# A gated cross-attention block: block 1's queries from a transposed copy in DRAM, quantized tokens transposed by TensorE, and a reordered start and end

## The chip, the cores and the metric

The kernel runs on one core of a Trainium2 chip. The metric is the time of one execution on the device, in microseconds (us). The engines work side by side and wait for one another through semaphores: TensorE (PE in the profile; PEld is its weight load), VectorE (DVE), ScalarE (ACT), GpSimd (POOL) and SyncE (SP), which here only issues transfers.

## What is computed

```python
# x: (2, 2048, 512), ctx: (2, 77, 512), all float32
n = layernorm(x)
q, k, v = n @ Wq.T + bq, ctx @ Wk.T + bk, ctx @ Wv.T + bv     # 16 heads of 32
a = softmax(q @ k.T / sqrt(32)) @ v
x = x + tanh(g_xattn) * (a @ Wo.T + bo)

def qlinear(x, w, b):            # one scale for a whole tensor
    sx, sw = max(abs(x)) / 127, max(abs(w)) / 127
    return (round(x / sx) @ round(w / sw).T + b) * (sw * sx)

h = gelu(qlinear(layernorm(x), w1, b1))      # 512 -> 2048
x = x + tanh(g_ffn) * qlinear(h, w2, b2)     # 2048 -> 512
```

A scale is the largest value over all tokens. So no token can be quantized before the attention of the last one is done, and the second layer can't begin before the last value of `h` is known.

## The kernel before

The 4096 tokens are cut into 8 blocks (`NB`) of 512 tokens (`TB`), each of 4 tiles of 128 (`NT`). Blocks 0 to 3 belong to the first batch entry, 4 to 7 to the second. Three stages follow each other: attention over all blocks, the first feed-forward layer over all blocks, the second over all blocks.

**Attention.** Its order is written out by hand for all five engines: each engine runs its instructions in the order of the source. A block has 8 steps `s`; one step handles one group of 4 heads and half of the block's tokens. In step `k = 8i + s` the loop at L805 does this: `shares` of step k+1 (sum of the exponentials, reciprocal, and on POOL the product `e*rs`, L566), the products that a table assigns to the step (`plan`, `second`, `begin`, `end`), `apply_v` for a finished group, `scores` of step k+2 with their minimum `mx` on DVE (L537), the 8 transposes `pta` of the step's `e` on PE (L577) with two copies by ACT, the exponentials of step k+2 on ACT (L548), and then other work: sums for the products, norms of later blocks, preparation of the weights w1 and w2 (`tasks`). The projections of queries and outputs use seven products of quarters (`unit_q`, `unit_o`) whose sums POOL makes; blocks 0 and 1 project their queries plainly (`project_q`, L350).

Where the queries come from: for block 0 and 1 `normalize` (L332) makes the normalized tokens `xn` on DVE and `transpose_x` (L339) turns them round on PE with a copy by ACT. From block 2 on the kernel loads the transposed input `xT` from DRAM and `scale_x` (L303) multiplies it on POOL by a row of 1/sigma; the mean is taken care of by `center_wq` (L324), which subtracts from wq its column means. The row takes a round trip: `write_row` (L290) writes the 512 values of `rstd` to DRAM from SP, `read_row` (L295) reads them back to all 128 partitions.

The start (L776 to L802): norms and transposes of block 0 tile by tile, with the keys of batch entry 0 (`project_k`, L232; `place_k`, L245, puts the four heads of a group with four small instructions into `kblk`), then queries, scores of steps 0 and 1, and the values (`project_v`). The keys and values of batch entry 1 follow in steps 3 to 6 of block 0 (L909). `bank` (L224) hands out two PSUM banks in turn (`pp0`, `pp1`) to `project_k`, `project_q`, `project_v`, `project_o` and `pm`: a new tile waits until the last reader of the tile before in its bank is done. Transfers go through SP's queue in order of the source. x, the raw weights and wk and wv share 8 buffers of 1 MB (`big`, L74), so the last of the four loads of w1 waits for the last use of wk (L236). POOL's first small instruction, `nbk` (L777), needs `bk`, and `inverse_sigma` (L170) runs behind it.

The end of attention: block 7 hands its work on by halves (`apply_v_half`, L597). Steps 5 to 7 project the outputs of tile 0, 1, and of tiles 2 and 3 in parts; behind the loop follow the last group, the extremes of each token (`extreme`, L642), the norms, and the common scale (`scale_of`, L185).

**First feed-forward layer** (L1014): for each block 16 chunks of 128 hidden units, 4 matmuls of 128x512 each in bf16 (L1031), one Gelu by ACT (L1039) out of four PSUM banks (`ps_h`), and one `tensor_reduce` by DVE for the largest value of each two chunks (L1049). `G` holds 4 chunks; there are 10 such tiles, the last 10 are kept, the others are stored to DRAM. Meanwhile `quantize_x` (L996) makes the next block's tokens: DVE normalizes, scales and rounds them (two tiles at a time) and DMA transposes (L1010), issued by SP, turn them round. Only PE's order is written by hand here; a scheduler places the rest.

**Second layer** (L1072): ACT and DVE quantize `h`, held or read back, PE multiplies (L1098), and the results go out.

Of the kernel before, what the change touches and what calls it, by code (L numbers as in the profile page):

```python
# [15 lines left out]
P = 128  # L16
D = 512
# [25 lines left out]
def tile_flamingo_gated_block(  # L43
# [88 lines left out]
    for g in range(2, NG):  # L132
        load_group(nc.sync, wq_sb, wqT, g)
    for b in range(1, B):
        load_ctx(nc.sync, b)
    load_x(1)
# [5 lines left out]

    nc.sync.dma_start(wo_sb, kchunks(woT))
# [10 lines left out]
    nc.vector.memset(ones, 1.0)  # L154
    mhalf = const.tile([P, NT], F32, name="mhalf")
# [6 lines left out]
    hmax = const.tile([P, NB * GT * 2 + 1], F32, name="hmax")  # L162
# [55 lines left out]
    with actx:  # L218
# [97 lines left out]
        def sum_columns(total):  # L316

            pm = bank("pm")
            nc.tensor.matmul(pm, ones, total, start=True, stop=True)
            mean = work.tile([P, D], F32, tag="rrow", name="wq_mean", bufs=1)  # L320
            nc.scalar.activation(mean, pm, AF.Copy, scale=1.0 / D)
            return mean
# [27 lines left out]
        def project_q(i, g):  # L350
            pq = bank(f"pq{i}_{g}")
            for kc in range(KC):
                nc.tensor.matmul(  # L353
                    pq,
                    wq_sb[:, kc, g * P : (g + 1) * P],
                    (xnT if i < 2 else xT_sb)[i][:, kc, :],
                    start=(kc == 0),
                    stop=(kc == KC - 1),
                )
            if g % 2 == 0:  # L360
                qT[i, g // 2] = work.tile([P, 2, TB], F32, tag="qT", name=f"qT{i}_{g}", bufs=2)
            q = qT[i, g // 2][:, g % 2, :]
            nc.scalar.activation(q, pq, AF.Identity, bias=bq_sb[:, g : g + 1])
# [149 lines left out]
        def part(i, s):  # L513


            return divmod(s, 2) if i + 1 < NB else (s % NG, s // NG)

        def scores(i, s):

            g, half = part(i, s)  # L520
            n = f"{i}_{s}"

            ps = ps_s.tile([P, NR, 512], F32, tag="ps", name=f"ps{n}")
            for u in range(2):
                t = 2 * half + u
                for q in range(NR):
                    r = slice(q * RT * DK, (q + 1) * RT * DK)
                    nc.tensor.matmul(  # L528
                        ps[:, q, u * RK : (u + 1) * RK],
                        qT[i, g // 2][r, g % 2, t * P : (t + 1) * P],  # L530
                        kblk[i // NBB][r, g, :],
                        start=True,
                        stop=True,
                    )
            mx = small.tile([P, NR, 2, RT], F32, tag="mx", name=f"mx{n}")
            sc = ps[:, :, : 2 * RK].rearrange("p q (u r k) -> p q u r k", u=2, r=RT)
            nc.vector.tensor_reduce(mx, sc, AX.X, ALU.min)  # L537
            scored[i, s] = sc, mx
# [58 lines left out]
        def apply_v_half(i, s):  # L597

            g, half = part(i, s)
            odd = s % 2  # L600
            pc = ps_t.tile([P, H], F32, tag="pt", name=f"pc{i}_{s}")
            for j in range(HG):
                r = slice(j * DK, (j + 1) * DK)
                c = g * P + j * DK
                nc.tensor.matmul(
                    pc[r, :],
                    vblk[i // NBB][:, c : c + DK],
                    aT[i, s // 2][:, j, odd * H : (odd + 1) * H],
                    start=True,
                    stop=True,  # L610
                )
            if s in (0, 2):
                cT[i, g // 2] = work.tile([P, 2, TB], F32, tag="cT", name=f"cT{i}_{g}", bufs=3)
            nc.scalar.copy(cT[i, g // 2][:, g % 2, half * H : (half + 1) * H], pc)
# [135 lines left out]
        begin = {1: ("", "p2"), 3: ("", "p3"), 5: ("", "P0"), 6: ("", "P1"), 7: ("", "P2")}  # L750
# [25 lines left out]
        nbk = small.tile([P, KC], F32, tag="nbk", name="nbk", bufs=1)  # L776
        nc.gpsimd.tensor_scalar(nbk, bk_sb, -SCALE, None, ALU.mult)  # L777
        pk = {}
        for t in range(NT + 1):
            if t < NT:  # L780
                norm_stats(0, t)
            if t > 0:
                normalize(0, t - 1)
                transpose_x(0, t - 1)
            if t in (2, 3):
                pk[t - 2] = project_k(0, t - 2)
        place_k(0, 0, pk[0])
        pk[2] = project_k(0, 2)
        place_k(0, 1, pk[1])
        project_q(0, 0)  # L790
        place_k(0, 2, pk[2])
        pk[3] = project_k(0, 3)
        place_k(0, 3, pk[3])
        load_x(2)
        for j in range(4):
            load_w("w1", j)
        for s in range(2):
            scores(0, s)
            exponential(0, s)
        project_q(0, 1)  # L800
# [4 lines left out]
        for i in range(NB):  # L805
# [3 lines left out]
            for s in range(2 * NG):  # L809
# [22 lines left out]
                if i == 0:  # L832
                    if s == 1:
                        total = sum_wq()
                    if s == 2:


                        nc.scalar.activation(tg, tg, AF.Tanh)
                        nc.gpsimd.tensor_scalar(bo_sb, bo_sb, tg[:, 0:1], None, ALU.mult)
                    if s in (5, 6):  # L840
                        for n in range(2):
                            sums_wq(2 * (s - 5) + n)
                    if s == 7:
                        for n in range(2):
                            sums_wo(n)
                if i == 1 and s in (1, 2):
                    sums_wo(s + 1)
                if i > 0 and s < 2:
                    for n in ((1, 2), (4,))[s]:
                        sums_c(i - 1, n)  # L850
                if more and i > 0:
# [5 lines left out]
                for t in range(NT):  # L857
                    if s == ((4, 5, 6, 7) if i == 0 else (4, 4, 5, 6))[t]:
# [4 lines left out]
                if i == 0 and s in (2, 3):  # L863
                    normalize(1, 2 * s - 4)
                    normalize(1, 2 * s - 3)
# [8 lines left out]
                if i > 0:  # L874
# [4 lines left out]
                    these = {5: (0,), 6: (1,), 7: (2,)} if more else {6: (0, 1), 7: (2,)}  # L879
# [11 lines left out]
                if not more and s > 4:  # L891

                    if s < 7:
                        project_o(i, s - 5)
                        later = [(add_o, i, s - 5), (norm2_stats, i, s - 5)]
                    else:
                        both = ps_s.tile([P, NR, 512], F32, tag="ps", name="po_last")
                        for these in (0, 1), (2,):
                            project_o(i, 2, these)
                            for n, c in enumerate(halves):  # L900
                                project_o(i, 3, these, c, psum=both[:, n, :])
                if i == 0 and s == 2:
                    mean = sum_columns(total)
                if i == 0 and s == 3:
                    center_wq(mean)
                if i == 0 and s in (3, 4):
                    transpose_x(1, 2 * s - 6)
                    transpose_x(1, 2 * s - 5)
                if i == 0 and 3 <= s < 7:  # L909
                    for b in range(1, B):  # L910
                        place_k(b, s - 3, project_k(b, s - 3))
                        if s == 6:
                            project_v(b)
                for task, args in tasks.get(k, ()):
                    task(*args)
                if i + 2 < NB:
# [8 lines left out]
        i, last = NB - 1, range(NG - 1, NG)  # L925
# [4 lines left out]
        project_o(i, 2, last)  # L930
        for c in halves:
            project_o(i, 3, last, c)
        for n in range(3, 2 * NT):
            extreme(i - 1, n)
        for t in range(2):
            norm2_max(i, t)
        add_o(i, 2)
        norm2_stats(i, 2)
        norm2_max(i, 2)
# [50 lines left out]
    with ExitStack() as fctx:  # L990
# [3 lines left out]
        )  # L994

        def quantize_x(i):  # L996

            xqT = xqT0
            if i % 2:
                xqT = fwork.tile([P, KC, TB], BF16, tag="xqT", name=f"xqT{i}", bufs=1)  # L1000
            n = NT // 2
            for t0 in range(0, NT, n):
                xs = fwork.tile([P, n, D], F32, tag="xs", name=f"xs{i}_{t0}")
                xq = fwork.tile([P, n, D], BF16, tag="xq", name=f"xq{i}_{t0}")
                for t in range(n):
                    normalize2(xs[:, t, :], i, t0 + t)
                quantize(xq, xs, inv_x)
                for t in range(n):
                    r = slice((t0 + t) * P, (t0 + t + 1) * P)
                    nc.sync.dma_start_transpose(xqT[:, :, r], xq[:, t, :])  # L1010
            return xqT

        fctx.enter_context(tc.manual_schedule(engines={mybir.EngineType.PE}))
        for i in range(NB):  # L1014
            cur = xqT if i else xqT0
            if i + 1 < NB:
                with tc.issue_after(last):
                    xqT = quantize_x(i + 1)
            for a in range(GT):
                G = gtile(f"G{i}_{a}")  # L1020
                for v in range(GF // 2):
# [24 lines left out]
                    k = (i * GT + a) * 2 + v  # L1046
                    n = 1 if k == NB * GT * 2 - 1 else 2
                    for u in range(0, 2, n):
                        nc.vector.tensor_reduce(  # L1049
                            hmax[:, k + u : k + u + 1],  # L1050
                            G[:, 2 * v + u : 2 * v + u + n, :],
# [136 lines left out]
```

## Time and profile before

| | us |
|---|---|
| median of 3 runs (630.91 to 632.41) | 631.1 |
| the profiled execution | 631.38 |
| its span, first to last instruction | 629.5 |
| PE busy | 596.9 (95%) |
| DVE busy | 478.3 (76%) |
| ACT busy | 411.3 (65%) |
| POOL busy | 330.6 (53%) |
| first matmul of the first layer | 396.4 |
| second layer at full pace | from 517.8 |

Busy time is the time in which an engine ran an instruction. It is an average over stages, and an engine that is busy is not for that the one that sets the end: that is read from the waits and from the chain that ended last, of which PE has 80%. A PSUM tile or an SBUF tile that is used again makes its writer wait for the last reader, so a wait can lead back through several engines.

### The profile page before, as it was taken

What the parts mean: (1) busy time and instruction counts of PE and PEld (TensorE: products, weight loads), DVE (VectorE), ACT (ScalarE), POOL (GpSimd) and SP (SyncE); (2) the same over time, 40 slices, a digit from 0 to 9 for tenths busy, and PEclk for the clock granted to TensorE, in tenths of its full rate; (3) what the DMA queues carried; (4) which work ended last, traced back from release to release, by engine and by line L of the source; (5) the groups of instructions that cost most, each with busy time, mean ns of one, the idle gap of its engine ahead of it and who ended that gap; (6) DMA issues with size and microseconds to landing.
All of it is one profiled execution on the core that took longest, in us unless ns stands there. A gap on an engine that the chain in (4) does not pass through costs nothing.

```text
span 629.5 us, 9452 instructions
## 1 busy us (share of the span) xinstructions
PE 596.9 (95%) x3322; PEld 370.1 (59%) x3322; DVE 478.3 (76%) x743; ACT 411.3 (65%) x926; POOL 330.6 (53%) x291
## 2 busy tenths in 40 slices
PE   3999999899999999999999997899999979999997
PEld 3556467677778777777777744344444424444444
DVE  4476658668998788778666868999999789877452
ACT  1377556777766867866766653698999879555620
POOL 3076687679777799697885462000000009997000
PEclk9999999999999999999999999799999989999999
DMA  9910350041360053240000040399998019798932
GB/s 288 374 54 1 135 133 18 1 151 67 134 218 1 18 180 124 84 168 1 17 1 1 2 151 0 108 334 342 342 345 232 1 60 376 272 367 320 399 127 83
DMA packets 51270, 94.95 MB, mean 151 GB/s; under 512 B 22219, under 2 KB 26571, under 8 KB 45464
## 3 DMA queue, kind: packets, MB, share of 16 engines
q1 hardware_dynamic: 50120, 93.67, 43.6%
q10 hardware_dynamic: 1104, 0.69, 0.4%
q8 instruction: 26, 0.43, 0.3%
q14 instruction: 20, 0.16, 0.2%
HBM read 57.11 MB, written 33.57 MB: 144 GB/s over the span
## 4 chain that ended last, share of the span: by engine, by line
PE 80%; DVE 9%; ACT 4%; POOL 4%; issue 1%; DMA 1%; ACTq 0%; POOLq 0%; DVEq 0%
PE ph L1031 18%; PE pf L1098 17%; PE pta L577 8%; PE oa L443 6%; PE ps L528 5%; PE qa L443 5%; PE ob L443 5%; PE qb L443 4%; PE pc L586 3%; PE pq L353 3%; ACT e L548 2%; PE po L621 2%; PE pvv L261 1%; POOL cs L380 1%; DVE sm L562 1%
## 5 line engine op out<-in xcount | busy, mean ns | idle before, releaser
L566 POOL TENSOR_TENSOR e<-e,rs 128x616 f32<-128x616 f32 x64 | 77.8, 1216 | 95.7 <-DVE rs L564 89.3
L548 ACT ACTIVATE e<-ps,mx 128x77 f32<-128x77 f32 x512 | 116.9, 343 | 9.9 <-DVE mx L537 9.7
L1098 PE MATMUL pf<-w2q,hq 128*128 128x512 bf16 (+1 forms) x528 | 112.4, 376 | 2.5 <-DVE hq L212 2.3
L1031 PE MATMUL ph<-xqT,w1q 128*128 128x512 bf16 x512 | 112.4, 383 | 1.8 <-DVE xqT L212 1.8
L1039 ACT ACTIVATE G<-ph,b1s,s 128x512 f32<-128x512 f32 x128 | 99.2, 777 | 13.6 <-PE ph L1031 2.9
L578 ACT COPY aT<-pta 77x512 f32<-77x512 f32 x128 | 68.8, 587 | 53.4 <-PE pta L577 53.4
L1098 PEld LDWEIGHTS <-hq 128*128 128x128 bf16 x528 | 51.8, 98 | 63.0 <-DVE hq L212 3.1
L1031 PEld LDWEIGHTS <-w1q 128*128 128x128 bf16 x512 | 50.5, 99 | 63.6 <-issue 4.3
L1049 DVE TENSOR_REDUCE hmax<-G 128x1 f32<-128x1024 f32 (+1 forms) x65 | 76.9, 1197 | 7.0 <-ACT G L1039 6.9
L577 PE MATMUL pta<-ident,e 128*77 128x128 f32 x512 | 71.2, 281 | 2.9 <-POOL e L566 1.3
L1089 POOL TENSOR_SCALAR b_sb<-b_sb,s 128x512 f32<-128x512 f32 x1 | 3.5, 3493 | 122.1 <-issue 122.1
L562 DVE TENSOR_REDUCE sm<-e 128x8 f32<-128x616 f32 x64 | 50.4, 787 | 22.7 <-ACT e L548 22.5
L537 DVE TENSOR_REDUCE mx<-ps 128x8 f32<-128x616 f32 x64 | 50.2, 785 | 22.7 <-PE ps L528 22.5
L1091 ACT ACTIVATE Gb<-Gb,inv_h 128x2048 f32<-128x2048 f32 x22 | 43.6, 2000 | 31.9 <-DMA Gb<-h 30.8
L577 PEld LDWEIGHTS pta<-ident,e 128*77 128x77 f32 x512 | 55.5, 147 | 14.8 <-issue 8.0
L528 PEld LDWEIGHTS ps<-kb,qT 64*128 64x128 f32 x512 | 36.0, 186 | 37.1 <-issue 31.4
L1112 POOL TENSOR_TENSOR x<-x,b_sb 128x512 f32<-128x512 f32 x32 | 57.2, 1825 | 0.1
L528 PE MATMUL ps<-kb,qT 64*128 64x154 f32 x512 | 50.6, 317 | 0.7 <-DVE qT L489 0.4
L1120 DVE SCALAR_TENSOR_TENSOR x<-pf,s,x 128x512 f32<-128x512 f32 (+1 forms) x33 | 23.7, 729 | 34.6 <-PE pf L1098 26.8
L647 DVE TENSOR_REDUCE xm<-x 128x1 f32<-128x512 f32 x64 | 40.8, 669 | 0.0
L348 POOL TENSOR_TENSOR x<-x,bo_sb 128x512 f32<-128x512 f32 x32 | 40.4, 1272 | 0.0
L1092 DVE TENSOR_SCALAR hq<-Gb 128x2048 bf16<-128x2048 f32 x22 | 36.5, 1701 | 1.2 <-ACT Gb L1091 1.1
(146 smaller groups left out, 939.9 us busy)
## 6 DMA issues: line engine op xcount, KB each, us to landing
h<-G SPq DMA_DIRECT2D x22, 1024.0 KB, 5.2
Gb<-h SPq DMA_DIRECT2D x22, 1024.0 KB, 7.8
out_y<-x SPq DMA_DIRECT2D x31, 256.0 KB, 3.1
x<-in_x SPq DMA_DIRECT2D x7, 1024.0 KB, 6.9
xT<-in_xT SPq DMA_DIRECT2D x6, 1024.0 KB, 9.0
raw_w<-in_w2T SPq DMA_DIRECT2D x6, 1024.0 KB, 6.6
raw_w<-in_w1T SPq DMA_DIRECT2D x4, 1024.0 KB, 12.5
w_dram<-xqT SPq DMA_DIRECT2D x4, 512.0 KB, 3.3
```

The source lines that it names most:

```text
L443: nc.tensor.matmul(ps[:, m * H : (m + 1) * H], a[:, c, m * P : (m + 1) * P], b[:, c, :], start=(m + c == 0 and not more), stop=(m + c == 2 ...
L528: nc.tensor.matmul(ps[:, q, u * RK : (u + 1) * RK], qT[i, g // 2][r, g % 2, t * P : (t + 1) * P], kblk[i // NBB][r, g, :], start=True, sto ...
L548: last = nc.scalar.activation(es[i, s][:, u, j * NK : (j + 1) * NK], sc[:, q, u, r, :], AF.Exp, bias=mx[:, q, u, r : r + 1], scale=-1.0,)
L562: nc.vector.tensor_reduce(sm, e4, AX.X, ALU.add)
L566: return nc.gpsimd.tensor_tensor(e4, e4, rs[:, :, :, None].to_broadcast([P, 2, HG, NK]), ALU.mult).ins
L577: nc.tensor.transpose(pt[:NK, j, :], es[i, s][:, u, j, :], ident)
L578: nc.scalar.copy(aT[i, g][:, :, t * P : (t + 1) * P], pt[:NK, :, :])
L1031: nc.tensor.matmul(ph[u], w1q[:, kc, fc * P : (fc + 1) * P], cur[:, kc, :], start=(kc == 0), stop=(kc == KC - 1),)
L1039: nc.scalar.activation(G[:, 2 * v + u, :], ph[u], AF.Gelu, bias=b1s[:, fc : fc + 1], scale=s1,)
L1049: nc.vector.tensor_reduce(hmax[:, k + u : k + u + 1], G[:, 2 * v + u : 2 * v + u + n, :], AX.XY, ALU.max, apply_absolute_value=True,)
L1098: nc.tensor.matmul(po[t, c.start][:, : c.stop - c.start], hq[:, fc, t * P : (t + 1) * P], w2q[:, fc, c], start=(fc == 0), stop=(fc == FC - 1),
L1112: nc.gpsimd.tensor_tensor(y, y, b2_sb, ALU.add)
```

## The change

It has these parts.

- Loads: `load_x(1)` is issued ahead of wq's groups 2 and 3, and the transposed tokens of block 1 (`load_xT(1)`) ahead of wo. The fourth load of w1 moves to the tasks of step 5.
- Start: 21 transposes `run_up` of the identity into a PSUM tile before anything else on PE, and 3 more behind block 0's first tile. `nbk` moves behind the loop over the tiles. Behind `place_k(0, 0)` come queries and scores; groups 1 to 3 of the keys are placed behind the scores of steps 0 and 1.
- Block 1: its queries come from `xT_sb`, scaled by `scale_x(1, kc)` in step 3, with `write_row(1)` in step 1 and `read_row(1)` in step 2. `normalize(1, ..)` and `transpose_x(1, ..)` are gone. `center_wq` moves from step 3 to step 2, the last `project_q` of block 0 too (`begin`). Keys and values of batch entry 1 are made in steps 3 and 4 in place of 3 to 6. `sums_wq` and `add_bias` of blocks 0 and 1 move to other steps.
- Block 7: steps 4 to 7 take two groups of heads for one tile in place of one group for two tiles (`part`), so that tile 2 is complete one step before tile 3. Tile 2's output is projected whole in step 7; the extremes of block 6 move from behind the loop into steps 4 and 5.
- First layer: `transpose_q` turns the quantized tokens round with PE's transposes in bf16, 8 for each half of a block, ahead of the matmuls of `a = 2` and `a = 3`, into one of two new PSUM banks (`ps_q`), and ACT copies each half with one instruction. The DMA transposes are gone. The largest value of `h` is taken once for 4 chunks, but for the last tile.

```diff
+    load_x(1)
     for g in range(2, NG):
         load_group(nc.sync, wq_sb, wqT, g)
...
-    load_x(1)
+    load_xT(1)
...
-                    (xnT if i < 2 else xT_sb)[i][:, kc, :],
+                    (xT_sb if i else xnT)[i][:, kc, :],
...
-            return divmod(s, 2) if i + 1 < NB else (s % NG, s // NG)
+            if i + 1 < NB:
+                return s // 2, 2 * (s % 2) + u
+            return (s, u) if s < NG else (2 * (s % 2) + u, s // 2)
...
-        begin = {1: ("", "p2"), 3: ("", "p3"), 5: ("", "P0"), 6: ("", "P1"), 7: ("", "P2")}
+        begin = {1: ("", "p2"), 2: ("", "p3"), 5: ("", "P0"), 6: ("", "P1"), 7: ("", "P2")}
...
-        nbk = small.tile([P, KC], F32, tag="nbk", name="nbk", bufs=1)
-        nc.gpsimd.tensor_scalar(nbk, bk_sb, -SCALE, None, ALU.mult)
+        run_up = ps_s.tile([P, KC, P], F32, tag="ps", name="run_up")
+        for n in range(21):
+            nc.tensor.transpose(run_up[:, n % KC, :], ident, ident)
...
+            if t == 1:
+                for n in range(3):
+                    nc.tensor.transpose(run_up[:, n, :], ident, ident)
             if t in (2, 3):
                 pk[t - 2] = project_k(0, t - 2)
+        nbk = small.tile([P, KC], F32, tag="nbk", name="nbk", bufs=1)
+        nc.gpsimd.tensor_scalar(nbk, bk_sb, -SCALE, None, ALU.mult)
         place_k(0, 0, pk[0])
-        pk[2] = project_k(0, 2)
-        place_k(0, 1, pk[1])
         project_q(0, 0)
-        place_k(0, 2, pk[2])
-        pk[3] = project_k(0, 3)
-        place_k(0, 3, pk[3])
         load_x(2)
-        for j in range(4):
+        for j in range(3):
             load_w("w1", j)
+        at(5, load_w, "w1", 3)
         for s in range(2):
             scores(0, s)
             exponential(0, s)
+        place_k(0, 1, pk[1])
+        for g in range(2, NG):
+            place_k(0, g, project_k(0, g))
         project_q(0, 1)
...
+                    if s == 3:
+                        for kc in range(KC):
+                            scale_x(1, kc)
...
-                    if s == ((4, 5, 6, 7) if i == 0 else (4, 4, 5, 6))[t]:
+                    if s == ((5, 5, 6, 6) if i == 0 else (5, 6, 6, 7) if i == 1 else (4, 4, 5, 6))[t]:
                         add_bias(i, t)
...
-                if i == 0 and s in (2, 3):
-                    normalize(1, 2 * s - 4)
-                    normalize(1, 2 * s - 3)
...
-                    these = {5: (0,), 6: (1,), 7: (2,)} if more else {6: (0, 1), 7: (2,)}
+                    these = {5: (0,), 6: (1,), 7: (2,)} if more else {4: (0, 1, 2, 3), 5: (4, 5, 6, 7)}
...
                 if i == 0 and s in (3, 4):
-                    transpose_x(1, 2 * s - 6)
-                    transpose_x(1, 2 * s - 5)
-                if i == 0 and 3 <= s < 7:
                     for b in range(1, B):
-                        place_k(b, s - 3, project_k(b, s - 3))
-                        if s == 6:
+                        for n in ((0, 1, 2), (3,))[s - 3]:
+                            place_k(b, n, project_k(b, n))
+                        if s == 4:
                             project_v(b)
...
+                if k == 1:
+                    write_row(1)
+                    at(k + 1, read_row, 1)
...
-                    nc.sync.dma_start_transpose(xqT[:, :, r], xq[:, t, :])
...
+        def transpose_q(xqT, i, half, xq):
+
+            r = slice(half * HT * P, (half + 1) * HT * P)
+            pt = ps_q.tile([P, KC, HT, P], BF16, tag="pq", name=f"ptq{i}_{half}")
+            for u in range(HT):
+                for kc in range(KC):
+                    nc.tensor.transpose(pt[:, kc, u, :], xq[:, u, kc * P : (kc + 1) * P], ident16)
+            pt = pt.rearrange("p k u t -> p k (u t)")
+            nc.scalar.copy(xqT[:, :, r], pt)
...
+                if a >= 2 and i + 1 < NB:
+                    transpose_q(xqT, i + 1, a - 2, xq[a - 2])
...
-                    k = (i * GT + a) * 2 + v
-                    n = 1 if k == NB * GT * 2 - 1 else 2
-                    for u in range(0, 2, n):
+                    final = (i, a) == (NB - 1, GT - 1)
+                    k = i * GT + a + (2 * v if final else 0)
+                    for n, part_of in (
+                        ((0, slice(2 * v, 2 * v + 2)),) if final and v == 0
+                        else ((0, slice(2, 3)), (1, slice(3, 4))) if final
+                        else ((0, slice(0, GF)),) if v else ()
+                    ):
```

## The prediction

> **What bounds the kernel now.** I read the busy time by stage first, then TensorE's list of waits, then the timeline of the stages that the change touches.
>
> ```profile
> 0.00:31.70 31.70, 21.42 (x96) 14.27 (x96) 13.22 (x35) 8.46 (x23) 7.02 (x19) 1.00 0.98 331
> 31.70:81.00 49.30, 46.03 (x261) 26.26 (x259) 32.89 (x60) 33.38 (x103) 34.15 (x30) 1.00 0.17 59
> 81.00:136.00 55.00, 52.70 (x324) 39.23 (x322) 39.72 (x70) 36.52 (x106) 41.86 (x37) 1.00 0.26 68
> ...
> 381.00:396.40 15.40, 8.68 (x47) 5.71 (x46) 12.56 (x30) 5.04 (x9) 2.39 (x6) 0.89 0.00 0
> 396.40:507.90 111.50, 111.50 (x509) 50.19 (x509) 103.35 (x123) 97.97 (x127) 0.00 (x0) 0.98 0.76 241
> ```
>
> Columns: stretch, length, then busy us of PE, PEld, DVE, ACT, POOL, the clock, DMA share, GB/s. PE is the bound nearly everywhere. In the first feed-forward layer (396.4 to 507.9) it has no gap at all: whatever PE is given there is paid in full, whatever is taken from the DMA there is worth nothing. Gaps to win lie in the prologue (10.3 us), blocks 0 and 1 (3.3 and 2.3) and the turn at 381 (6.7).
>
> ```profile
> PE ptx L344 <- DVE xn L335: 10.1, 1, 10.1
> ...
> PE ph L1031 <- DVE xqT L212: 1.8, 1, 1.8
> PE qa L443 <- POOL xt L380: 1.6, 1, 1.6
> ```
>
> These are who PE waits for, with total us, times, longest: one long wait at the start, one of 1.6 us in block 1, and in L1031 only the first.
>
> **Prologue.** The timeline of before:
>
> ```profile
> 8.30 0.23 POOL L777 TENSOR_SCALAR nbk<-bk_sb 128x4 f32<-128x4 f32 x1 [5.90 <-DMA bk_sb<-in_bk]
> 9.54 0.55 DVE L335 TENSOR_SCALAR xn<-x,mv,rstd 128x512 f32<-128x512 f32 x1 [3.93 <-POOL rstd L175]
> 12.30 1.83 PE L236 MATMUL pk<-ctx,wk_sb 128*128 128x77 f32 x8
> 18.25 3.64 PE L353 MATMUL pq<-xnT,wq_sb 128*128 128x512 f32 x8
> 21.73 1.01 PE L236 MATMUL pk<-ctx,wk_sb 128*128 128x77 f32 x8
> 24.03 1.51 DVE L537 TENSOR_REDUCE mx<-ps 128x8 f32<-128x616 f32 x2
> 30.98 0.79 PE L528 MATMUL ps<-kb,qT 64*128 64x154 f32 x8
> ```
>
> nbk holds Pool, and rstd behind it, until bk lands. Moved behind the loop, rstd follows mv (4.82) by 0.24 + 0.57, so xn0 starts at 5.8 and xn3 ends 4.4 later as before, at 10.2. The same pk work takes 1.83 us at 12.3 and 1.01 at 21.7: PE runs at half speed until about 17.3, some 7 us after its first work at 10.14. The 21 run_up transposes start when ident is ready (1.9) and at the slow pace (four ptx in 0.9) end at 6.6. Full speed 7 us after 2 gives: ptx0 7.5, three more 8.2, ptx1 9.1, pk0 10.1, ptx2 10.6, pk1 11.6, ptx3 12.2, copy 0.6: pq0 at 12.8, against 18.25. Bounds: 11.9 if fast from 6.6, 15.2 if slow throughout.
>
> [...]
>
> But 5.4 us at pq0 don't reach the loop. The two banks of ps_p go in turn: pk2 takes the one of pk1, whose four place_k copies now stand behind both score minima on DVE. From pq0's start: scores 4.4 to 5.7, minima 5.3 to 6.8, place_k(0,1) 1.22 to 8.0, pk2 to 9.05, its copies to 10.3, and pq1, which takes that bank, 10.4 to 13.85, pvv, and scores 2 at 17.35 (before: 12.73). So scores 2 start at 30.15, not 30.98: 0.8 us won (1.9 won to 1.5 lost).
>
> **Block 0.** Removed: 16 ptx (0.13 each, 2.1 us of PE), four normalize, four copies; pk and pvv of the second batch move up. Added: four scale_x (1.27 each) on Pool behind a round trip through DRAM, and Pool multiplies e behind them. The DMA queue of before:
>
> ```profile
> 116.74 0.37 SPq L293 DMA_DIRECT2D row<-rstd  x1
> 125.12 0.34 SPq L299 DMA_DIRECT2D rrow<-row  x1
> ...
> 249.90 0.54 SPq L293 DMA_DIRECT2D row<-rstd  x1
> 261.90 0.34 SPq L299 DMA_DIRECT2D rrow<-row  x1
> ```
>
> The read is issued when the write has landed: 8.4 us in a quiet queue, 12 beside a load; the read lands in 3.3 to 5.9. xT1 (1 MB, 2.9 us at the 360 GB/s of then) goes early and the loads end at about 37, so I take 8.4 and 3.3 to 4.6. w1's fourth load no longer blocks SP until L236 is done with wk (70.6), or the write couldn't be issued. Counted from scores 2: step 0 and 1 as before, rstd at 11.9, pq3 10.4 to 13.9, mean at 15.4, center on Pool (4 x 1.33) to 20.75, e4 to 22.0; scales in hand at 23.7 to 25.1; scale_x 5.05 to 28.8 or 30.2; e5 1.22. PE runs pta3, three pk (the third waits for a bank to 19.85), pc, scores 6, pta4, pk, pvv and scores 7 to 28.8 and waits for e5 until 30.1 to 31.5: a new wait of 1.3 to 2.7 us. pq0 of block 1 starts at 31.8, or 61.95 (before 58.25). Up to the end of pq3 before took 27.1 us with two pk and a pvv (5.4) that are now done: 21.7, so 83.65 against 85.35: 1.7 us won by here (3.4 won to 2.9 lost: both bounds of the start, round trip up to 12 + 5.9).
>
> **Block 1 and the tail.** Two add_bias (2.49 together) leave the place ahead of xt2, for which PE waited 1.6: 1.4 won (0 to 1.6). Blocks 2 to 6 have PE busy to within 0.5 us each: the shift is carried. In the last block the reordered tokens leave PE the same work; eight extremes (0.64 each) move from the end into steps 4 and 5, where they make e7 and pta7 0.5 late, and afterwards three tokens' (3.85) still stand before the last add: the chain on DVE ends 0.8 earlier (1 lost to 1.3 won).
>
> **First feed-forward layer.** 28 DMA transposes go: worth nothing, PE didn't wait for them. PE gets 7 x 16 transposes of 128x128 in bf16; no row has one. Bounds from rows:
>
> ```profile
> L1031 PE MATMUL ph<-xqT,w1q 128*128 128x512 bf16 x512 | 112.4, 383 | 1.8 <-DVE xqT L212 1.8
> L1031 PEld LDWEIGHTS <-w1q 128*128 128x128 bf16 x512 | 50.5, 99 | 63.6 <-issue 4.3
> L1039 ACT ACTIVATE G<-ph,b1s,s 128x512 f32<-128x512 f32 x128 | 99.2, 777 | 13.6 <-PE ph L1031 2.9
> 74.86 1.03 PE pta L577 x8
> ```
>
> The last line is from the chain. Below: a quarter of ph's 0.216 (110.64 / 512), 0.054 or 6.0 us. Above: the f32 transpose of the same size, 1.03 / 8 = 0.129 or 14.4; or each bound by its weight load, 0.099 or 11. An f32 matmul takes twice a bf16 one per column (256 columns in 0.216), so I take half of 0.129: 0.064, 7.2 us lost. None is hidden. [...]
>
> ACT gets 14 copies of 128x1024. From 0.379 for 256 columns and 0.587 for 512 one takes 1.0. Per block ACT then has 16 x 0.777 + 2.0 = 14.4 us, PE 13.8 + 1.0 = 14.85: PE stays the bound as long as a copy is under 1.2. A copy delays the next gelu by some 0.5, which four ph banks (1.8 us) hide. DVE's 65 reduces become 35 of up to twice the size: 4 to 5 us of DVE saved, off the path; xq is made nearly a block ahead. The second layer is unchanged.
>
> **Sum.** -1.7 - 1.4 - 0.8 + 7.2 = +3.3. The profiled execution took 631.38 (span 629.5, 1.9 around it): 634.7; the median shown is 0.3 lower, so I say 634.5, slower.
>
> **Rivals.** (1) Not slower: the early start reaches the loop. If pk2 and pq1 don't wait for the banks (scores 2 at pq0 + 12.7), 4.6 more is won: 629.9. For it: pq0's inputs really are earlier; against: pq0 itself waited for a place_k in before (17.87, then 18.18). It decides if scores 2 start before 26.9. (2) The transposes are bound by their weights, 0.099 to 0.129: 638.3 to 641.7; for: f32 pk with 77 columns takes as long per pass as with its weights alone (0.126); against: bf16 weights show half of f32's time. (3) The round trip meets loads, 12 + 5.9: pta5 waits 3 us more, 637.5. (4) run_up doesn't do what it says, and the clock stays low: 636.9.
>
> **Numbers.** Forecast 45%, (1) 23%, (2) 12%, (3) 10%, (4) 10%. A difference under 0.3% (1.9 us) can't be told from none. (1) splits: 12 faster, 11 same; of the forecast's own range (631.5 to 637) 10 are same. So faster 0.12, same 0.21, slower 0.67. Range 629.8 to 640: it leaves out the far end of (2) and the near one of (1).
>
> **What would show it.** Right: pq0 near 12.8 but scores 2 near 30; PE waiting for DVE kb before pk2 and for Pool's e before pta5; pta5 near 60; ph's stretch 7 us longer with PE still full. Wrong: scores 2 before 27; eight ptq taking 0.8 us or more; ACT without gaps in that stretch.

## The result and the profile after

The changed kernel takes 635.36 us (median of 14 runs, 634.35 to 639.47), the kernel before 631.62 (14 runs beside them): a ratio of 1.0065, 95% interval 1.0052 to 1.0078. It is slower, by 3.7 us. The forecast was 634.5. The profiled execution took 634.79 with a span of 633.0.

The same points of the work in both profiled executions tell where the time went:

| point (us from the start) | before | after | shift | of it in this stage |
|---|---|---|---|---|
| first matmul of block 0's queries (pq0) | 18.25 | 11.86 | -6.39 | -6.39 |
| scores 2 | 30.98 | 30.60 | -0.38 | +6.01 |
| end of block 1's queries (first oa) | 85.34 | 85.27 | -0.07 | +0.31 |
| second oa of block 1 | 136.05 | 134.81 | -1.24 | -1.17 |
| first ph of the first layer | 396.40 | 393.40 | -3.00 | -1.76 |
| end of its last ph | 508.75 | 511.95 | +3.20 | +6.20 |
| product for the scale of h (pg_h) | 510.92 | 514.54 | +3.62 | +0.42 |
| end of the span | 629.5 | 633.0 | +3.5 | -0.1 |

Of blocks 2 to 6 nothing is seen: the eight pta near the end of block 6 start at 338.63 against 339.89, 1.26 earlier, so their part of the fifth row is 0.02. The stages as they were read before, in the changed kernel (busy time by stage: stretch, length, busy us of PE, PEld, DVE, ACT, POOL, the granted clock, DMA share, GB/s):

```profile
0.00:31.30 31.30, 25.51 (x120) 17.19 (x120) 13.22 (x35) 8.57 (x23) 7.41 (x20) 0.95 1.03 324
31.30:81.10 49.80, 46.79 (x246) 26.66 (x245) 28.43 (x57) 31.54 (x99) 39.67 (x35) 0.93 0.27 92
81.10:134.80 53.70, 52.52 (x322) 39.06 (x321) 39.65 (x70) 36.52 (x106) 40.65 (x36) 1.00 0.26 69
379.85:393.40 13.55, 8.38 (x54) 5.80 (x53) 10.71 (x26) 5.04 (x9) 2.39 (x6) 1.00 0.00 0
393.40:511.95 118.55, 118.55 (x624) 56.62 (x623) 102.74 (x92) 108.50 (x142) 0.00 (x0) 0.99 0.48 195
```

Two things are new here. In the first layer PE still has no gap, with 118.55 us where it had 112.35 for the same ph: what it was given there it paid in full. (Both stretches begin at half clock, for 3.4 and 3.3 us, so the clock makes no difference between them.) And in the first two rows PE's clock, 1.00 before, is 0.95 and 0.93. The list of PE's waits, where 10.1 for xn has gone:

```profile
PE pk L240 <- issue: 2.4, 1, 2.4
...
PE pk L240 <- ACT kb L257: 1.7, 1, 1.7
PE pta L582 <- POOL e L571: 1.3, 2, 0.7
...
PE qa L447 <- POOL xt L384: 0.5, 1, 0.5
```

The first two are new. For the first the list names nobody ("issue"); that it is the wait for the bank of pk1 is shown below by keys_first, where it is gone. The second is the wait of the third pk of the second batch entry for its bank. The third row reads the same in the kernel before, but the wait of 0.66 that stood at 44.15 there is now one of 0.69 at 63.34, at the last pta ahead of block 1's queries. The fourth was 1.6 before.

**Start.** PE in the timeline:

```profile
1.96 4.74 PE L789 MATMUL run_up<-ident 128*128 128x128 f32 x21 [1.96 <-POOL ident masks.py:199]
6.60 1.11 PE L348 MATMUL ptx<-ident,xn 128*128 128x128 f32 x4
...
7.89 0.62 PE L348 MATMUL ptx<-ident,xn 128*128 128x128 f32 x4
8.35 1.01 PE L240 MATMUL pk<-ctx,wk_sb 128*128 128x77 f32 x8
...
11.86 3.70 PE L357 MATMUL pq<-xnT,wq_sb 128*128 128x512 f32 x8 [0.68 <-ACT xnT L349]
16.34 1.32 PE L533 MATMUL ps<-kb,qT 64*128 64x154 f32 x16 [0.78 <-ACT qT L367]
20.04 2.55 PE L240 MATMUL pk<-ctx,wk_sb 128*128 128x77 f32 x16 [2.38 <-issue]
22.49 4.75 PE L357 MATMUL pq<-xnT,wq_sb 128*128 128x512 f32 x8
...
30.60 0.79 PE L533 MATMUL ps<-kb,qT 64*128 64x154 f32 x8
```

The reader sees full speed from about 7.4: ptx0 in 1.11, ptx1 in 0.62. All that PE had done by then was transposes. Then, after 2.38 us of standing still, it is lost again: pq in 4.75 at 22.49, in 3.70 at 11.86, with the same eight matmuls.

**Block 0.** The DMA queue, then GpSimd's timeline:

```profile
42.70 0.37 SPq L297 DMA_DIRECT2D row<-rstd  x1
50.99 0.34 SPq L303 DMA_DIRECT2D rrow<-row  x1
51.43 0.38 SPq L136 DMA_DIRECT2D xT<-in_xT  x1
```

```profile
57.18 4.93 POOL L310 TENSOR_TENSOR xT<-xT,rrow 128x512 f32<-128x512 f32 x4 [5.03 <-DMA rrow<-row]
62.08 1.21 POOL L571 TENSOR_TENSOR e<-e,rs 128x616 f32<-128x616 f32 x1
```

A row of 2 KB is written (8.3 us), read back (6.2), then four chunks are scaled, then e5, the exponentials of step 5, is multiplied and ready at 63.3. PE reaches pta5, their transposes, only 0.69 us before it, since it ran at half clock from about 52 to 58.8. Block 1's first pq starts at 64.28. So POOL's chain ends block 0, and PE is close to it.

**First layer.** Two rows of ScalarE (busy us, mean ns, idle us before), then the line of the chain in which eight transposes take 0.45 us:

```profile
L1061 ACT ACTIVATE G<-ph,b1s,s 128x512 f32<-128x512 f32 x128 | 97.9, 780 | 10.1 <-PE ph L1053 2.9
...
L1028 ACT COPY xqT<-ptq 128x1024 bf16<-128x1024 bf16 x14 | 14.0, 1002 | 0.0
```

```profile
402.10 0.45 PE ptq L1026 x8
```

14 times 0.45 is 6.3. ScalarE's copy takes 1.00 us; its gaps (10.1 us) remain.

### The profile page after: what moved, and what is told of

Read it like the earlier page. It is cut to its first block, busy times and chain, and to the rows that moved or that the text cites. A ratio compares the mean times of both kernels' runs of the same rounds, so it can differ in the third digit from the quotient of the medians.

```text
span 633.0 us, 9673 instructions
## 1 busy us (share of the span) xinstructions
PE 607.7 (96%) x3474; PEld 380.1 (60%) x3474; DVE 472.4 (75%) x709; ACT 419.2 (66%) x936; POOL 335.2 (53%) x296
## 4 chain that ended last, share of the span: by engine, by line
PE 86%; DVE 6%; ACT 3%; POOL 3%; issue 1%; POOLq 0%; DVEq 0%; ACTq 0%
PE ph L1053 17%; PE pf L1124 17%; PE pta L582 9%; PE oa L447 7%; PE ps L533 6%; PE qa L447 5%; PE ob L447 5%; PE pq L357 5%; PE pc L591 4%; PE qb L447 4%; ACT e L553 2%; PE po L631 2%; PE pk L240 1%; POOL cs L384 1%; PE ptq L1026 1%
## 5 line engine op out<-in xcount | busy, mean ns | idle before, releaser
L1053 PE MATMUL ph<-xqT,w1q 128*128 128x512 bf16 x512 | 114.6, 383 | 1.8 <-DVE xqT L216 1.8
L1061 ACT ACTIVATE G<-ph,b1s,s 128x512 f32<-128x512 f32 x128 | 97.9, 780 | 10.1 <-PE ph L1053 2.9
L1075 DVE TENSOR_REDUCE hmax<-G 128x1 f32<-128x2048 f32 (+2 forms) x34 | 73.0, 2155 | 12.0 <-ACT G L1061 12.0
```

Source lines behind the costliest of these rows:

```text
L1053: nc.tensor.matmul(ph[u], w1q[:, kc, fc * P : (fc + 1) * P], cur[:, kc, :], start=(kc == 0), stop=(kc == KC - 1),)
L1061: nc.scalar.activation(G[:, 2 * v + u, :], ph[u], AF.Gelu, bias=b1s[:, fc : fc + 1], scale=s1,)
L1075: nc.vector.tensor_reduce(hmax[:, k + n : k + n + 1], G[:, part_of, :], AX.XY, ALU.max, apply_absolute_value=True,)
```

## The experiments

Times are medians; "before" beside them is the kernel before on the same chip at the same time (631.35 to 631.66). The changed kernel was not run again beside them: what is said against it goes by its 635.36 above. The edits are against the changed kernel where nothing else is said, and marked "..." where they are shortened.

### dma_transposes: the first layer as before

```diff
+                    nc.sync.dma_start_transpose(xqT[:, :, r], xq[:, t, :])
...
-                if a >= 2 and i + 1 < NB:
-                    transpose_q(xqT, i + 1, a - 2, xq[a - 2])
```

> The changed kernel with the DMA transposes of before in the first feed-forward layer; everything else stays. Theory (TensorE's 112 transposes are paid in full, some 0.056 us each, and nothing else of that layer is lost but 0.4 us at its end): first ph matmul at 393.4 as in the changed kernel, the stretch of ph 6.3 us shorter, time 635.4 - 6.3 = 629.1, faster than both kernels. Rival (the layer is longer because ScalarE's copies or the longer maxima hold TensorE up, and the transposes are half of it at most): 632 or more with the copies' share told by ScalarE's gaps. Rival 2 (the changes ahead of the layer give nothing that lasts): 631.6, as before.

Measured: 631.16 (629.56 to 633.21, 12 runs), ratio 0.9993 (0.9981 to 1.0004). The profiled execution took 630.02, span 627.6: first ph at 393.31, last ph's end at 505.54, a stretch of 112.23 instead of 118.55. So the transposes are the whole of the 6.3 us of that layer, as the theory has it. The time as a whole missed its 629.1: the medians differ by 4.2. In this profile 0.7 us were given back at the start of the second layer, where the clock stood at half for 6.8 us and not 3.4; what the higher of the twelve runs lost no trace shows.

### before_pe_transposes: TensorE's transposes in the kernel before

```diff
# against the kernel before
-                    xqT = quantize_x(i + 1)
+                    xq = [quantize_x(i + 1, half) for half in range(2)]
...
+                if a >= 2 and i + 1 < NB:
+                    transpose_q(xqT, i + 1, a - 2, xq[a - 2])
```

> The kernel before with TensorE's transposes and ScalarE's copies in the first feed-forward layer and nothing else. Theory: 631.6 + 6.3 = 637.9, and eight transposes of one half in 0.45 us. Rival (half of the loss is of other parts of the change): 634.5 to 635.

Measured: 637.07 (636.95 to 637.25), ratio 1.0088 (1.0075 to 1.0101): 5.4 us slower than before. Eight ptq take 0.45 us here too. The rival with half the loss is out. (In the profiled execution pq0 came 1.4 us earlier than in that of before, at 16.88: 0.4 because PE's first input was there earlier, at 9.75 and not 10.14, the rest because PE got to full speed earlier: its second pk took 1.12 us, 1.82 in before.)

### hmax_two: maxima over two chunks

```diff
-                        else ((0, slice(0, GF)),) if v else ()
+                    for u in range(0, 2, n):
...
+                            G[:, 2 * v + u : 2 * v + u + n, :],
```

> The changed kernel with the maxima over two chunks at a time, as before. Theory (the last reduce of four chunks stands 2.3 us ahead of the final ones): end of the maxima 0.4 us nearer to TensorE's end, 635.0; TensorE's stretch unchanged. Rival (fewer, longer reduces give VectorE room that the layer needs): longer stretch of ph, over 636.

Measured: 635.72 (634.69 to 637.26): the time can't tell. The profile can: ph's stretch is 118.64 (118.55), and pg_h follows its end by 2.17 us, as before, not by 2.59. The last maxima in VectorE's timeline, of the changed kernel first:

```profile
509.35 4.60 DVE L1075 TENSOR_REDUCE hmax<-G 128x1 f32<-128x2048 f32 x4 [1.17 <-ACT G L1061]
```

and of this run:

```profile
511.36 2.41 DVE L1070 TENSOR_REDUCE hmax<-G 128x1 f32<-128x1024 f32 x3 [0.51 <-ACT G L1060]
```

In the first a reduce of four chunks, 2.29 us long, still runs when the first values of the last tile are there, and the last four maxima, this one among them, end at 513.95, 2.0 us after ph; in the second the last three end 1.5 us after it (513.77, ph's end 512.24). The 0.4 is shown, and VectorE's saved time is worth nothing.

### no_run_up: without the transposes of the identity

```diff
-        for n in range(21):
-            nc.tensor.transpose(run_up[:, n % KC, :], ident, ident)
...
-                for n in range(3):
-                    nc.tensor.transpose(run_up[:, n, :], ident, ident)
```

> The changed kernel without the 21 and the 3 transposes of the identity. Theory (transposes alone bring the clock up, 5.5 us after the first): first ptx at 6.6 as now, but slow up to about 12, pq0 at about 14.1 instead of 11.9; the bank wait at pk2 stays, so up to 2.2 us later at scores 2 and 635.4 to 637.6. [...]

Measured: 639.39 (637.36 to 640.01), ratio 1.0116 (1.0102 to 1.0131), 4.0 us over the changed kernel. PE in its timeline:

```profile
6.57 2.37 PE L348 MATMUL ptx<-ident,xn 128*128 128x128 f32 x8 [6.57 <-DVE xn L339]
8.73 1.83 PE L240 MATMUL pk<-ctx,wk_sb 128*128 128x77 f32 x8
...
14.56 6.34 PE L357 MATMUL pq<-xnT,wq_sb 128*128 128x512 f32 x8 [0.68 <-ACT xnT L349]
```

The inputs come at the same time (6.57), a pk takes 1.83 us instead of 1.01, and the slow pace lasts into pq, 6.34 instead of 3.70: pk2 starts at 25.38, 5.3 us later than with run_up. With run_up PE was at full speed from about 7.4, when it had done nothing but transposes. The loss was higher than expected because the clock came some 13 us after the first work and not 5.5.

### keys_first: no wait for the bank at pk2

```diff
         place_k(0, 0, pk[0])
+        place_k(0, 1, pk[1])
         project_q(0, 0)
...
-        place_k(0, 1, pk[1])
         for g in range(2, NG):
```

> The changed kernel with the placing of keys 1 put ahead of the two score minima on VectorE, so that the bank of the third keys is free when TensorE gets there. Theory (the wait of 2.4 us at pk2, and the half clock that follows it, hold the early start back): pk2 at 17.7 behind scores 1, scores 2 at 26.9 instead of 30.6, and most of these 3.7 us carried through block 0: 632 (631.7 to 633). Rival (my third one: the round trip of rstd through DRAM ends block 0, and an earlier write falls among the loads): the wait moves to GpSimd's e ahead of pta5, 0 to 1.5 us won, 634 to 635.4.

Measured: 632.72 (631.62 to 635.47), ratio to before 1.0024 (1.0008 to 1.0039): 2.6 us under the changed kernel. PE's timeline:

```profile
17.51 2.01 PE L240 MATMUL pk<-ctx,wk_sb 128*128 128x77 f32 x16
19.99 3.67 PE L357 MATMUL pq<-xnT,wq_sb 128*128 128x512 f32 x8 [0.47 <-PE pk L240]
...
27.02 0.79 PE L533 MATMUL ps<-kb,qT 64*128 64x154 f32 x8
...
60.32 1.10 PE L582 MATMUL pta<-ident,e 128*77 128x128 f32 x8 [2.92 <-POOL e L571]
61.26 3.60 PE L357 MATMUL pq<-xT,wq_sb 128*128 128x512 f32 x8
```

Scores 2 come 3.6 us earlier, and 3.0 of them are there at block 1's pq. The wait at pta5 grew from 0.69 to 2.92: the chain through DRAM (row written at 39.10, read at 47.97, scaled from 54.16, e5 at 60.3) moves with the start and sets the end of block 0. So the theory is right in its main point, the time at the upper part of its range, and its rival in where the next limit is.

### filled_wait: the wait kept, the clock held

```diff
+        fill = ps_t.tile([P, KC, P], F32, tag="pt", name="fill")
+        for n in range(20):
+            nc.tensor.transpose(fill[:, n % KC, :], ident, ident)
         place_k(0, 1, pk[1])
```

> The changed kernel with 20 more transposes of the identity in the wait ahead of pk2; the wait itself stays. They fill 2.2 of its 2.4 us. Theory (the clock falls since TensorE stands still, and 1.8 us are lost at pk2, pk3 and pq1 by that): pk2 and pk3 in 1.9, pq1 in 3.5 us, scores 2 at about 28.8 instead of 30.6, of which 1.8 or less arrive at the end: 633.6 to 635.4. Rival (the slow pace there is of something else, as of the transfers that run beside it): scores 2 at 30.6 to 30.8, pk2 and pk3 in 2.5 as now.

Measured: 636.14 (635.15 to 637.46), no better than the changed kernel. But at its place it did what the theory says, in PE's timeline:

```profile
17.70 2.40 PE L815 MATMUL fill<-ident 128*128 128x128 f32 x20
20.15 1.98 PE L240 MATMUL pk<-ctx,wk_sb 128*128 128x77 f32 x16
22.60 3.67 PE L357 MATMUL pq<-xnT,wq_sb 128*128 128x512 f32 x8 [0.47 <-PE pk L240]
...
29.63 0.79 PE L533 MATMUL ps<-kb,qT 64*128 64x154 f32 x8
```

pk and pq run at full speed (two pk in 1.98 us, not 2.55, pq in 3.67, not 4.75; the granted clock from 20 to 24 is 1.00, 0.66 in the changed kernel) beside transfers of much the same rate (374 and 385 GB/s), so the slow pace was the clock's fall while PE stood still, not the loads. That is worth 1.0 us at scores 2 (1.8 was reckoned: pq1 now waits 0.47 for its own bank), and of it 0.2 are left at block 1's pq (64.10), since the round trip of the row took 15.3 us this time and not 14.5. Holding the clock alone pays nothing; the wait has to go.

### block0_repaired: the second bank wait and the load beside the read

```diff
# with the edit of keys_first
-                        for n in ((0, 1, 2), (3,))[s - 3]:
+                        for n in ((0, 1), (2, 3))[s - 3]:
                             place_k(b, n, project_k(b, n))
...
-                    if s == 4:
+                    if s == (5 if i == 0 else 4):
                         load_xT(i + 2)
```

> The changed kernel with keys 1 placed early, the second batch entry's keys two and two in steps 3 and 4 (no wait of 1.7 us for the bank of the third), and block 2's transposed tokens loaded a step later, behind the reading of block 1's row. Theory (the two bank waits and the half clock behind them cost block 0 its gain): no half clock before 380, row read landed 3 to 4.6 us after its issue, block 1's first pq at 58.7 to 60 instead of 64.4, time 630 to 631.5. Rival (the round trip is what ends block 0): pq at 62 to 64, 633 to 635.

Measured: 632.05 (631.33 to 633.56), ratio 1.0010 (0.9999 to 1.0021): 0.5 over what the theory gave, and under the rival. Block 1's pq starts at 60.85, 0.4 before keys_first, and not at 58.7 to 60. The read, with no load behind it, still took 5.3 us (48.41 to 53.75; 6.2 with the load), and the bank wait moved to the values, in PE's timeline:

```profile
48.81 1.10 PE L582 MATMUL pta<-ident,e 128*77 128x128 f32 x8 [1.68 <-POOL e L571]
...
53.55 5.36 PE L265 MATMUL pvv<-wv_sb,ctx 128*77 128x512 f32 x8 [1.91 <-ACT kb L257]
```

pvv takes 5.36 instead of 3.60: here too a stretch at half clock follows (0.59 granted from 54 to 58), which the theory had ruled out.

### repaired_dma: the same with the old first layer

The edits of block0_repaired, dma_transposes and hmax_two together.

> The kernel of the run before this one with the DMA transposes of before and the maxima over two chunks: all the edits that shorten the attention, without the one that lengthens the feed-forward layer. Theory (the parts add up): 630 to 631.5 less 6.3 and 0.4: 623.5 to 625, some 7 us under the kernel before. Rival (DMA transposes meet what the earlier start brings with it): over 627.

Measured: 625.62 (625.45 to 625.79), ratio 0.9905 (0.9886 to 0.9924). It beats both kernels, by 5.8 and 9.7 us, and is 6.4 under block0_repaired, where 6.7 were expected of transposes and maxima; that is 0.6 above the theory's range and below the rival. The parts of the change that touch the attention are worth some 6 us, once the wait ahead of pk2 is gone; the part that touches the first layer costs as much.

### repaired_dma_split and values_first: two tries at what is left of block 0

```diff
# with the edits of repaired_dma
+                        if s == 4:
+                            project_v(b)
                         for n in ((0, 1), (2, 3))[s - 3]:
                             place_k(b, n, project_k(b, n))
-                        if s == 4:
-                            project_v(b)
...
# repaired_dma_split alone: chunks 2 and 3 at the end of step 4
+            engine = nc.vector if i == 1 and kc > 1 else nc.gpsimd
```

> The repaired kernel with DMA transposes, and block 0 once more: values of the second batch entry ahead of keys 2 and 3 in step 4 (so that their product doesn't wait 1.9 us for a bank), and two of the four chunks of block 1's tokens scaled by VectorE at the end of step 4. Theory (the end of block 0 is GpSimd's chain: row landed 53.5, four chunks 4.9, e5 1.2): e5 ready at 57.3, pta5 at 57.3 instead of 59.7, pq of block 1 at 58.3, 623.2. Rival (what is left is TensorE's own work): pta5 no earlier than 59, 625 to 625.6. Rival 2 (VectorE, waiting for the row, holds up minima and shares behind it): over 626.

> The repaired kernel with DMA transposes, and of the last run's two edits only the first: the second batch entry's values are multiplied ahead of keys 2 and 3. Theory (with all four chunks on GpSimd, its chain sets the end of block 0: row landed at 52.8 to 53.5, 4.9, 1.2): no wait of 1.9 us at pvv, pta5 at 58.9 to 59.6 behind a wait for GpSimd's e of 2.5 to 3.5 us, nothing held up on VectorE, 624.8 to 625.6. Rival (the split run lost by the order of keys and values, not by VectorE's chunks): 626 or more.

Measured: 626.65 (626.19 to 627.0) and 626.3 (624.84 to 627.13), neither better than repaired_dma. By the times the split run fits its rival 2 and values_first its rival, and the two can't be told apart; what each lost is read from its trace. In the split run pq starts at 57.45, 3.2 us earlier than in repaired_dma and 0.8 earlier than expected, and loses it again at once: VectorE's two chunks and a weight maximum put off the minima and shares behind them, PE waits 2.25 us for qT at 64.29, and pta behind it runs at half speed, 1.99 us instead of 1.10. In values_first the wait at pvv became one at pta5, and PE ran at half speed after that (pta in 1.99, pq in 4.13 instead of 3.60). PE's timeline there:

```profile
59.30 1.99 PE L581 MATMUL pta<-ident,e 128*77 128x128 f32 x8 [3.17 <-POOL e L570]
61.08 4.13 PE L356 MATMUL pq<-xT,wq_sb 128*128 128x512 f32 x8
```

With four chunks on GpSimd pta5 starts, as the theory says, only 0.4 earlier (59.72 in repaired_dma): the chain through DRAM sets it. The time still isn't the theory's, and the half speed behind the wait is what it left out.

### tail_undone: the last block as before

```diff
-            return (s, u) if s < NG else (2 * (s % 2) + u, s // 2)
+            return s % NG, 2 * (s // NG) + u
...
-                    these = {5: (0,), 6: (1,), 7: (2,)} if more else {4: (0, 1, 2, 3), 5: (4, 5, 6, 7)}
+                    these = {5: (0,), 6: (1,), 7: (2,)} if more else {6: (0, 1), 7: (2,)}
...
+        project_o(i, 2, last)
...
+        add_o(i, 2)
+        norm2_stats(i, 2)
+        norm2_max(i, 2)
```

> The changed kernel with the last block's order of tokens, its extremes and its end as before. Theory (the last token's sums no longer stand behind token 2's add, statistics and extremes, 2.8 us of VectorE, but behind TensorE alone): the first ph matmul 1.85 us later against po of that block than now, at about 395.2 instead of 393.4, and 637.2. Rival (my prediction: only 0.8 of it): 636.2. Rival 2 (the shift came from the blocks ahead, and the tail gives nothing): 635.4, ph at 393.4.

Measured: 637.75 (637.12 to 638.29), 2.4 us over the changed kernel. From the outputs of tile 1 to the first ph it takes 22.59 us (373.17 to 395.76), as before (22.58), against 20.74 in the changed kernel (372.66 to 393.40): 1.85. VectorE's timeline of this run:

```profile
385.95 0.75 DVE L641 SCALAR_TENSOR_TENSOR x<-po,tg,x 128x512 f32<-128x512 f32 x1 [1.38 <-PE po L631]
...
387.56 1.25 DVE L657 TENSOR_REDUCE xm<-x 128x1 f32<-128x512 f32 x2
388.73 0.47 DVE L641 SCALAR_TENSOR_TENSOR x<-po_last,tg,x 128x256 f32<-128x256 f32 x1
```

Between PE's last product for token tile 2 and the last tile's add stand its add, its statistics and two extremes, 2.8 us of VectorE. In the changed kernel:

```profile
381.54 0.75 DVE L641 SCALAR_TENSOR_TENSOR x<-po,tg,x 128x512 f32<-128x512 f32 x1 [3.19 <-PE po L631]
...
383.15 3.62 DVE L657 TENSOR_REDUCE xm<-x 128x1 f32<-128x512 f32 x6
386.68 0.47 DVE L641 SCALAR_TENSOR_TENSOR x<-po_last,tg,x 128x256 f32<-128x256 f32 x1
```

Tile 2's add is 4.4 us earlier, and six extremes now stand between it and the last add, which follows them without idle time. PE's last product ends at 386.21, so VectorE's chain and PE's end within half a microsecond of each other, and the theory's "behind TensorE alone" is not what the rows show. From tile 1's outputs the last add comes 1.54 earlier than in this run. The other 0.3 of the 1.85 lies behind it, in pg_x (the product for the scale of x): 0.80 us here and 0.49 in the changed kernel, where the half clock came only after it, at 393.31. The rest of the 2.4 is not the tail's: in the profiles 0.5 is there ahead of it (373.17 against 372.66).

## Why the prediction held

The sum was +3.3 and the profiled spans differ by +3.5. The main step is shown: the transposes cost what a gapless stage charges for them, and the start's gain doesn't get through. But that the sum fits so closely is luck. Block 0 brought 1.6 less than reckoned, block 1 0.2 less and the maxima cost 0.4; the tail brought 1.0 more and the first layer cost 1.0 less.

- **pq0 at 12.8 (11.9 to 15.2): 11.86.** run_up does bring the clock, in this profile some 5.4 us after it starts, where I took 7 from the one start that I had; other starts in these runs show from about 5 (before_pe_transposes) to 13 (no_run_up). Rival 4 would have cost more than its 636.9: without run_up 639.4.
- **Scores 2 at 30.15: 30.60.** The step "pk2 waits for the bank of pk1" is right to 0.2 us (pk2 8.2 behind pq0, reckoned 8.0). The clock's fall behind that wait was not in it; filled_wait prices it at 1.0. That pq0 came 0.9 earlier than reckoned hid most of it.
- **Block 0, 1.7 won: 0.07.** This term failed. Its mechanism held, POOL's chain through DRAM ends the block, but the read was taken as 3.3 to 4.6 us and took 6.2. Writing took the 8.3 that was reckoned. With scores 2 0.45 late, e5 was ready at 63.3, reckoned for 60.25 to 61.65, and block 1's first pq came at 64.28, reckoned for 61.95; 0.7 of that was won back behind it. The load issued behind the read is part of it: without it the read took 5.0 to 5.5 us in four profiles, with it 5.9 to 6.2 in six, but 5.0 in no_run_up. So even a read alone takes longer than was reckoned. PE's half clock cost PE about 3.4 us in this stretch (6.8 at half) but lay beneath that chain: that is why the new wait was 0.69 and not 1.3 to 2.7.
- **Rival 1** (the early start reaches the loop, from scores 2 before 26.9): keys_first makes nearly that, at 27.02, and takes 632.7, not 629.9, since the row's round trip comes next. In the changed kernel it didn't occur: the bank does hold it back.
- **Block 1, 1.4 won: 1.17.** The wait for xt fell from 1.6 to 0.5.
- **Tail, 0.8 won: 1.76.** The order was right: three tiles' extremes, 3.62 us, do stand ahead of the last add. Too small was how far tile 2's add moves: it comes 8.9 us behind the start of tile 1's products and not 12.8, and the extremes run while PE still multiplies. The last add is 1.5 earlier by that. Another 0.3 is the clock's: pg_x took 0.49 and not 0.79, and that is luck. In dma_transposes and hmax_two, where it takes 0.80, the way from tile 1's outputs to the first ph is 21.04 and not 20.74.
- **First layer, 7.2 lost (6.0 to 14.4): 6.2.** A bf16 transpose took 0.056 us, not the 0.064 between the rows; nearly the lower bound, a quarter of ph's time for 512 columns. It isn't bound by its weights (0.099), so rival 2 is out. PE stayed the bound, as said, with copies of 1.00 us.
- **End of the maxima, taken as nothing: 0.4 lost.** "Off the path" was true for all reduces but the last of four chunks.

## What to carry to other kernels

An engine that is the bound of a stage pays for every instruction it is given there; work moved onto it from a DMA that nobody waited for is a loss, however small the single instruction (here 112 transposes of 0.056 us, 6.3 us together). An early start is only worth what the next wait lets through (here 6.39 us at pq0 and 0.38 at scores 2), so the pools' turns and a round trip through DRAM should be followed up to the end of the stage before the gain is put into a sum. And a wait of TensorE can cost more than its length: after it the same matmuls may run at half speed, here for 3.4 or 6.8 us.

## What was unexpected of the hardware

**The clock falls after short waits, and where a wait lies counts as well as its length.** Where PE stood still for 1.91 us (block0_repaired, repaired_dma), 2.25 (repaired_dma_split), 2.38 (the changed kernel, no_run_up) or 3.17 (values_first) in the attention of these runs, a stretch at half speed followed, and after 1.72 us in the changed kernel and 1.70 in keys_first too. None followed 1.68 us at 48.81 in block0_repaired, nor the 2.92 us in keys_first (pta at 60.32 takes 1.10, pq behind it 3.60). In the changed kernel half speed begins at 21.26, 51.98, 393.31 and 516.19 and lasts 3.41 us, from 51.98 on 6.83; in thousandths each of these stretches is 3.413 us or twice that, and the last three lie 9, 109 and 145 times 3.413 us behind the first. Cut at steps of 3.413 us, the changed kernel reads (the columns are those of the stages above; the clock is the third number from the end):

```profile
17.85:21.26 3.41, 1.23 (x11) 1.25 (x12) 2.11 (x7) 3.25 (x16) 0.00 (x0) 1.00 1.14 321
21.26:24.68 3.42, 3.42 (x10) 2.29 (x10) 3.05 (x9) 0.32 (x2) 0.00 (x0) 0.50 1.05 385
...
48.57:51.98 3.41, 1.69 (x15) 1.23 (x17) 1.16 (x4) 2.16 (x9) 3.41 (x3) 1.00 0.00 0
51.98:55.40 3.42, 3.42 (x21) 1.97 (x14) 2.10 (x5) 1.22 (x3) 0.18 (x1) 0.50 0.13 51
55.40:58.81 3.41, 3.41 (x15) 2.81 (x15) 0.28 (x1) 2.89 (x10) 1.63 (x2) 0.50 0.82 307
```

and keys_first, in its own steps:

```profile
55.55:58.96 3.41, 1.85 (x11) 0.71 (x9) 2.25 (x3) 0.32 (x1) 3.41 (x3) 1.00 0.92 349
58.96:62.38 3.42, 2.06 (x11) 1.51 (x12) 3.25 (x8) 1.33 (x4) 3.42 (x4) 1.00 0.00 0
62.38:65.79 3.41, 3.41 (x16) 0.93 (x14) 1.53 (x3) 2.25 (x9) 3.41 (x4) 1.00 0.00 0
```

A step's length less PE's busy time is the time PE stood still in it. In the changed kernel it is 2.2 and 1.7 us, and the next step is at half. In keys_first the 2.92 us fall into two steps, 1.6 and 1.4, and nothing follows. In the traces of the changed kernel and of the kernel before, from the time that PE first reached full speed, no step at full speed with 1.67 us or less of standing still was followed by half speed, and each with 1.72 or more was. Near these values the amount alone doesn't decide: in keys_first some 1.6 us, of the wait that ends at 46.94, were followed by half speed from about 48.7 (worked out from a granted clock of 0.73 from 50 to 54), and the 1.6 above were not. By these figures the same wait costs more or less by where it lies. This is read from the traces; no run moved a wait within its step. Why half speed lasts one step or two is open: from 51.98 to 58.81 PE had no gap.

**The clock at the start isn't shown.** The granted clock of the first 31 us of the kernel before stands at 1.00, though its first pk took 1.83 us and a later one 1.01: here the pace of like instructions has to be read at the start, not the clock.

**How long the first half speed lasts changes.** From PE's first work to full speed it took 5.4 us in the changed kernel, about 7 in the kernel before, about 5 in before_pe_transposes, which has the same start, and 13 without run_up. Why no_run_up took so long is open.

**Runs of one kernel spread differently.** repaired_dma and before_pe_transposes (5 and 4 runs) lie within 0.4 us, the changed kernel (14) within 5.1, dma_transposes (12) within 3.7 and hmax_two (5) within 2.6. What decides that is open; one profile for each kernel can't show it. The mean clock of a run alone doesn't: among the runs of the changed kernel 634.35 and 637.64 both had 0.986.
